# Tiles of 32 rows by 128 columns in place of 32 by 32 for two thin products of an RWKV block

## The chip, the cores and the metric

The kernel runs on one core of a Trainium2 chip. The metric is the device time of one execution, in microseconds (us); the number given for a kernel is the median of its runs. The engines of the core are called by the profile's names: PE (TensorE, matrix products; PEld are its weight loads), DVE (VectorE), ACT (ScalarE), POOL (GpSimd) and SP (SyncE, which issues DMA transfers).

## The reference

The reference is one block of an RWKV-6 layer in float32, for 8 sequences of 256 tokens with 512 channels. What matters here is the part ahead of the scan:

```python
xn = _ln(x, ln1_w, ln1_b)
sx = _token_shift(xn, state[:, i1])
xxx = jnp.tanh((xn + sx * maa_x) @ maa_w1).reshape(b, l, 5, 1, EXTRA_MAA)
xxx = jnp.matmul(xxx, maa_w2).reshape(b, l, 5, E)
x5 = xn[:, :, None] + sx[:, :, None] * (maa_stack + xxx)
w = jnp.exp(-jnp.exp(time_decay + jnp.tanh(x5[:, :, 1] @ decay_w1) @ decay_w2))
r = (x5[:, :, 3] @ Wr.T).reshape(b, l, H, S)
k = (x5[:, :, 0] @ Wk.T).reshape(b, l, H, S)
v = (x5[:, :, 2] @ Wv.T).reshape(b, l, H, S)
g = jax.nn.silu(x5[:, :, 4] @ Wg.T)
```

There are five mixes, the "mix groups". Each has its own 32 hidden channels (EXTRA_MAA = 32) and its own matrix `maa_w2[g]` of 32 x 512. So the product behind the tanh is thin: it sums over 32 channels and yields 512. After this part come a scan over the tokens with a 16 x 16 state in each of 32 heads, a group norm, the gate, the product with Wo, and a feed-forward block.

## The kernel before, in words

Channels lie on the 128 partitions and tokens along the free axis, so a sequence is four blocks of 128 channels by 256 tokens, held as two tiles (q = 0, 1) of two blocks (m = 0, 1). For every sequence b there are three stages: `inputs_of_scan` (normalising, mixing, projections), `scan`, and `rest`. Stages of neighbouring sequences overlap.

The code doesn't issue instructions directly. It adds pieces of work to a plan (`Plan.add`), each with an engine, an assumed time, the buffers that it writes and reads, and a function that issues it. `Plan.order` sorts the pieces by a list of ranks written out by hand (`TURNS`), assumed times and free buffers, and fixes for each engine the order of its pieces and for each piece its buffers. After that the order on every engine is static. On PE a piece also has a mode: "rows32", "rows64", "columns", "turn" (transposes) or "any". The mode of the neighbours decides for an "any" piece whether it is issued as four matmuls of 128 rows by 32 columns (`narrow`) or as one of 128 by 128. There are six general PSUM tiles (`ps`) of 128 partitions by 512 float32.

The helper `mul` (line 395; its matmul is line 398, which is the line that the profile shows for nearly all products) splits a product of 128 output channels into pieces of n columns of weights:

```python
def mul(out, w, x, first=True, final=True, tiles=None):
    n = 32 if (narrow if tiles is None else tiles) else P
    for i in range(0, P, n):
        nc.tensor.matmul(out[i : i + n], lhsT=w[:, i : i + n], rhs=x, start=first, stop=final)
```

Three callers set `tiles`, so that they always use 32 columns, whatever the mode:

- `mixed` (line 653, the product at line 667) makes four of the five mixes. The weights `mw2a` hold group g on the partitions 32g to 32g + 31; the tanh output `ta` has the same layout. For each q there is one piece ("rows32", assumed 0.875 us): for both m and the four groups 1, 0, 2, 3, one product with 32 rows, four matmuls each, 32 matmuls of 32 rows by 32 columns by 256 tokens. Each group writes a PSUM tile of its own, so a piece needs four of them. After it, for b > 0, ACT adds the group's bias in PSUM (line 674), DVE multiplies by the token shift `sx` (line 676) and POOL adds `xn` (line 686). For b = 0, where nothing else is running yet, DVE does bias and product in one instruction (line 680), and two of the PSUM places come from the wide buffer `wrep`.
- `mixed_last` (line 692, the product at line 700) makes the fifth mix. Its weights `mw2b` are four copies of the group's matrix, one in each quarter of the partitions, so that the four blocks k can use four quarters: one piece of 16 matmuls of 32 by 32 by 256 (assumed 0.45 us), into four PSUM tiles.
- The decay product (line 743, "rows64") has 64 rows: 16 matmuls of 64 by 32 by 256.

Two other pieces appear in the prediction. Line 862 gathers the scan's output (matmuls of 128 by 32), after which DVE adds it (line 868). Line 903 occurs only in the last sequence: for both m and both q one matmul of 64 rows by 128 columns by 256 tokens, issued directly and not through `mul`.

Of the kernel before, what the change touches and what calls it, by code (L numbers as in the profile page):

```python
# [12 lines left out]
P = 128  # L13
# [324 lines left out]
def tile_rwkv_block(  # L338
# [33 lines left out]
    def const(name, shape):  # L372
        return plan.fixed(sb.tile(shape, F32, tag=name, name=name), name)
# [8 lines left out]
    def new(pool, name):  # L382
        return Buf(pool, name, VIEWS.get(pool, lambda t: t))
# [6 lines left out]
    def pe(us, outs, ins, emit, mode="any", into=()):  # L390
        plan.add("PE", us, outs, ins, emit, mode, into)

    narrow = False

    def mul(out, w, x, first=True, final=True, tiles=None):
        n = 32 if (narrow if tiles is None else tiles) else P
        for i in range(0, P, n):
            nc.tensor.matmul(out[i : i + n], lhsT=w[:, i : i + n], rhs=x, start=first, stop=final)  # L398

    def act(n, out, ins, emit, table=None, pointers=0):  # L400
        plan.add("ACT", 0.1 + n * 0.00084 + 0.09 * pointers, [out], ins, emit, table)

    def dve(n, outs, ins, emit, each=1.05):
        plan.add("DVE", 0.065 + n * each / 1e3, outs, ins, emit)

    def gp(n, out, ins, emit, each=1.86):
        plan.add("POOL", 0.1 + n * each / 1e3, [out], ins, emit)
# [3 lines left out]
    w1, w2a, w2b = const("mw1", [P, NK, 6 * MAA]), const("mw2a", [P, E]), const("mw2b", [P, E])  # L411
    dw1, dw2 = const("dw1", [P, NK, DEC]), const("dw2", [2 * DEC, E])
# [37 lines left out]
    def col(name, k):  # L450
        i = VECS.index(name)
        return vec()[:, k, i : i + 1]
# [17 lines left out]
    def pieces(tiles):  # L470
        return [Part(t, lambda t, i=i: t[:, i, :]) for t in tiles for i in range(2)]
# [140 lines left out]
    def project(w, src, q, name, into):  # L612

        ps = new("ps", name)
        for m in range(2):
            o = (2 * q + m) * P

            def mm(m=m, o=o):
                for k in range(NK):
                    mul(ps()[:, m, :], w[k]()[:, o : o + P], src[k // 2]()[:, k % 2, :], k == 0, k == NK - 1)  # L620

            pe(1.728, [ps], [*w, *src], mm, into=[into])
        return ps

    def project_tokens(w, src, n, name, into):

        ps = new("ps", name)
        for h in range(2):

            def mm(h=h):  # L630
                for k in (2 * h, 2 * h + 1):
                    mul(ps().rearrange("p m t -> p (m t)"), src[h]()[:, k % 2, n * P : (n + 1) * P], w[k](), k == 0, k == NK - 1)

            pe(1.72, [ps], [*src, *w], mm, into=[into])
        return ps

    def inputs_of_scan(b, got):
        xn, sx = normed(load_x(b, "xt"), 1, 1, b, b == 0)
        xin = shifted(xn, sx, "maa_x", f"xin{b}", b == 0)
        px, ta, tb = new("ps", f"psx{b}"), new("ta", f"ta{b}"), new("tb", f"tb{b}")  # L640
# [3 lines left out]
        for ks in turns:  # L644

            def mm(ks=ks):
                for k in ks:
                    mul(px()[:, 0, :], w1()[:, k, 0:P], xin[k // 2]()[:, k % 2, :], k == begin, k == end)

            pe(0.432 * len(ks), [px], [w1, *dict.fromkeys(xin[k // 2] for k in ks)], mm, into=[ta])  # L650
        act(256, ta, [px], lambda: nc.scalar.activation(ta(), px()[:, 0, :], AF.Tanh), "exp")

        def mixed():

            groups = (1, 0, 2, 3)
            x5 = {g: [new("mix", f"x5_{b}_{g}_{q}") for q in range(NQ)] for g in groups}
            ps = {(g, q): new("ps", f"psm{b}_{g}_{q}") for g in groups for q in range(NQ)}
            if b == 0:
                wide = new("wrep", f"psm{b}")
                ps.update({(g, 0): Part(wide, lambda t, i=i: t[:, 2 * i : 2 * i + 2, :]) for i, g in enumerate(groups[:2])})  # L660
            for q in range(NQ):

                def mm(q=q):
                    for m in range(2):
                        for g in groups:
                            rows, k = slice(g * MAA, (g + 1) * MAA), 2 * q + m
                            mul(ps[g, q]()[:, m, :], w2a()[rows, k * P : (k + 1) * P], ta()[rows, :], tiles=True)

                pe(0.875, [ps[g, q] for g in groups], [ta, w2a], mm, "rows32", [x5[g][q] for g in groups])
                for g in groups:  # L670
                    t, p_ = x5[g][q], ps[g, q]
                    if b:
                        for m in range(2):
                            act(256, p_, [p_, vec], lambda g=g, q=q, m=m, p_=p_: nc.scalar.activation(  # L674
                                p_()[:, m, :], p_()[:, m, :], AF.Identity, bias=col(f"maa_{g}", 2 * q + m)), pointers=1)
                        dve(512, [t], [p_, sx[q]], lambda q=q, t=t, p_=p_: nc.vector.tensor_tensor(
                            t(), p_(), sx[q](), ALU.mult))
                    else:
                        for m in range(2):
                            dve(256, [t], [p_, vec, sx[q]], lambda g=g, q=q, m=m, t=t, p_=p_: nc.vector.scalar_tensor_tensor(  # L680
                                t()[:, m, :], p_()[:, m, :], col(f"maa_{g}", 2 * q + m), sx[q]()[:, m, :], ALU.add, ALU.mult), 1.28)
                    if b == 0 and g == 2:
                        dve(512, [t], [t, xn[q]], lambda q=q, t=t: nc.vector.tensor_tensor(
                            t(), t(), xn[q]()[:, :, 1 : T + 1], ALU.add))
                    else:
                        gp(512, t, [t, xn[q]], lambda q=q, t=t: nc.gpsimd.tensor_tensor(  # L686
                            t(), t(), xn[q]()[:, :, 1 : T + 1], ALU.add))
            if b == 0:
                dve(4, [wide], [], lambda: nc.vector.memset(wide()[:, :, 0:1], 0.0))
            return x5  # L690

        def mixed_last():

            ts = [new("mix", f"x5_{b}_4_{q}") for q in range(NQ)]
            ps = [new("ps", f"psm{b}_4_{k}") for k in range(NK)]

            def mm():
                for k in range(NK):
                    rows = slice(k * MAA, (k + 1) * MAA)
                    mul(ps[k]()[:, 0, :], w2b()[rows, k * P : (k + 1) * P], tb()[rows, :], tiles=True)  # L700

            pe(0.45, ps, [tb, w2b], mm, "rows32", ts)
            for q, t in enumerate(ts):
                for m in range(2):
                    k, p_ = 2 * q + m, ps[2 * q + m]
                    if b:
                        act(256, p_, [p_, vec], lambda k=k, p_=p_: nc.scalar.activation(
                            p_()[:, 0, :], p_()[:, 0, :], AF.Identity, bias=col("maa_4", k)), pointers=1)
                        dve(256, [t], [p_, sx[q]], lambda q=q, m=m, t=t, p_=p_: nc.vector.tensor_tensor(
                            t()[:, m, :], p_()[:, 0, :], sx[q]()[:, m, :], ALU.mult))  # L710
                    else:
                        dve(256, [t], [p_, vec, sx[q]], lambda q=q, m=m, k=k, t=t, p_=p_: nc.vector.scalar_tensor_tensor(
                            t()[:, m, :], p_()[:, 0, :], col("maa_4", k), sx[q]()[:, m, :], ALU.add, ALU.mult), 1.28)
                gp(512, t, [t, xn[q]], lambda q=q, t=t: nc.gpsimd.tensor_tensor(t(), t(), xn[q]()[:, :, 1 : T + 1], ALU.add))
            return {4: ts}

        x5 = mixed()
        pd, hd = new("ps", f"psd{b}"), new("w", f"w{b}_0")
# [18 lines left out]
        pw = [new("ps", f"psw{b}_{q}") for q in range(NQ)]  # L737

        def mm():
            for m in range(2):  # L740
                for q in range(NQ):
                    rows, k = slice(DEC * q, DEC * q + DEC), 2 * q + m
                    mul(pw[q]()[:, m, :], dw2()[rows, k * P : (k + 1) * P], hd()[rows, 1, :], tiles=True)

        pe(0.875, pw, [dw2, hd], mm, "rows64", ws)
        for q in range(NQ):
# [14 lines left out]
        if b == 0:  # L761
# [3 lines left out]
            for m in range(2):  # L765
                ps, vo = new("ps", f"psv{b}_0_{m}"), new("vo", f"vo{b}_0_{m}")
# [17 lines left out]
        for q in range(NQ):  # L784
            t = got["g", q] = new("g", f"g{b}_{q}")
            ps = project(pieces(W["g"]), x5[4], q, f"psg{b}_{q}", t)
# [215 lines left out]
    with tc.manual_schedule():  # L1002
        for op in plan.order(phases):
            narrow = op.narrow
# [75 lines left out]
```

## Time and profile before

| | |
|---|---|
| median of 3 runs | 622.74 us (622.51 to 624.09) |
| profiled execution, span from first to last instruction | 620.2 us |
| PE / PEld busy in that span | 599.9 / 344.8 us |
| DVE / ACT / POOL busy | 543.5 / 513.0 / 518.7 us |
| granted TensorE clock, mean | 0.999 |
| matmul records on PE | 8496 |

The profile shows one execution; its time is given as the span, and what lies around the span (launch and end) is the difference to the measured time. "128*32 128x256" behind a matmul reads: 128 rows and 32 columns of weights, and a moving operand of 128 partitions by 256 elements. Every float32 matmul of the code leaves two MATMUL and two LDWEIGHTS records. A row of the timeline has the start, the length and what ran; consecutive records of one kind are merged, with their count behind an x, and in brackets stands how long the engine was idle before them and what ended that. Because matmuls are pipelined, the length of a merged row runs past the start of the next; the distance between starts is the better measure. A row of the windows has the stretch, its length, then for each engine its busy time and the number of its instructions in that stretch, the granted clock, the DMA engines' busy share and GB/s.

### The profile page before, as it was taken

To read this page: it belongs to the slowest core of one execution; us is meant where nothing else is said; L and a number is where in the kernel's file an instruction comes from. 1 tells how busy PE (TensorE), PEld (TensorE's weight loads), DVE (VectorE), ACT (ScalarE), POOL (GpSimd) and SP (SyncE) were. 2 spreads that over 40 slices of the span, in tenths; PEclk is the share of its full clock that TensorE was granted. 3 is DMA by queue.
4 is the path that set the end of the run, shared out by engine and by line. 5 is a ranking of instruction groups with operands and counts; after the bars stand their busy time and mean duration, and the time that the engine had idled before them with its cause. 6 is when DMAs were issued, how large, how long until landed. Compare 5 with 4: busy or idle time off the path is not lost.

```text
span 620.2 us, 20062 instructions
## 1 busy us (share of the span) xinstructions
PE 599.9 (97%) x8496; PEld 344.8 (56%) x8496; DVE 543.5 (88%) x490; ACT 513.0 (83%) x1164; POOL 518.7 (84%) x414
## 2 busy tenths in 40 slices
PE   5999999899999999999999999999999999999997
PEld 5675656456534664357543665475754464547464
DVE  5689999899999999799889999999998999895441
ACT  3888679989999999989999888899889789965441
POOL 1799999899989998899889999989889998887030
PEclk9999999999999999999999999999999999999999
DMA  8896769596768678758687797687866698961542
GB/s 294 261 247 165 216 178 230 145 246 171 208 190 237 199 194 227 197 154 226 193 248 195 220 227 201 167 240 216 223 182 193 185 248 218 262 195 65 168 141 85
DMA packets 52504, 124.91 MB, mean 201 GB/s; under 512 B 5824, under 2 KB 11200, under 8 KB 52416
## 3 DMA queue, kind: packets, MB, share of 16 engines
q1 hardware_dynamic: 48048, 119.46, 70.0%
q10 hardware_dynamic: 4368, 4.20, 2.1%
q8 instruction: 66, 1.08, 0.8%
q14 instruction: 22, 0.18, 0.1%
HBM read 115.25 MB, written 8.39 MB: 199 GB/s over the span
## 4 chain that ended last, share of the span: by engine, by line
PE 72%; ACT 13%; DVE 6%; issue 3%; DMA 2%; POOL 2%; SPq 0%; ACTq 0%; DVEq 0%; POOLq 0%
PE ps L398 60%; PE ps L862 7%; DVE st L851 3%; PE ps L574 2%; ACT sq L917 2%; DMA Ws<-in_wo 2%; PE ps L726 2%; ACT rk L917 1%; DVE vs L849 1%; ACT L787 1%; ACT mix L605 1%; DMA Ws<-in_wv 1%; POOL st L854 1%; ACT att L812 1%; ACT vs L842 1%
## 5 line engine op out<-in xcount | busy, mean ns | idle before, releaser
L851 DVE TENSOR_TENSOR_SCAN st<-wrep,vs 128x1024 f32<-128x1024 f32 x128 | 289.6, 2281 | 4.4 <-ACT wrep L832 1.2
L854 POOL TENSOR_TENSOR st<-st,r 128x1024 f32<-128x1024 f32 x128 | 254.4, 2003 | 12.1 <-DVE st L851 11.8
L849 DVE TENSOR_TENSOR vs<-vs,ps 128x1024 f32<-128x1024 f32 x122 | 144.0, 1210 | 10.5 <-ACT vs L842 9.2
L398 PE MATMUL ps<-Ws,mix 128*32 128x512 f32 (+2 forms) x864 | 114.9, 589 | 1.0 <-ACT o L952 0.7
L398 PEld LDWEIGHTS ps<-Ws,mix 128*32 128x32 f32 (+1 forms) x864 | 37.9, 116 | 64.6 <-issue 58.9
L686 POOL TENSOR_TENSOR mix<-mix,xn 128x512 f32<-128x512 f32 x62 | 66.5, 1092 | 4.1 <-DVE mix L680 2.2
L588 POOL TENSOR_TENSOR sx<-xn 128x512 f32<-128x512 f32 x30 | 31.7, 1068 | 37.7 <-ACT xn L584 37.6
L862 PE MATMUL ps<-st,con 128*32 128x256 f32 x1024 | 61.7, 380 | 0.1
L398 PE MATMUL ps<-mix,Wr 128*32 128x256 f32 (+1 forms) x760 | 59.7, 380 | 0.9 <-issue 0.9
L398 PE MATMUL ps<-mix,Wv 128*32 128x256 f32 (+1 forms) x688 | 59.7, 380 | 0.0
L398 PE MATMUL ps<-mix,Wk 128*32 128x256 f32 (+1 forms) x952 | 58.6, 379 | 0.2 <-ACT tb L734 0.2
L398 PE MATMUL ps<-Ws,g 128*32 128x512 f32 (+1 forms) x464 | 56.7, 593 | 2.0 <-POOL g L928 1.6
L398 PE MATMUL ps<-mix,Wg 128*32 128x256 f32 (+1 forms) x712 | 58.5, 379 | 0.0
L398 PE MATMUL ps<-mix,Ws 128*32 128x256 f32 (+1 forms) x736 | 57.7, 380 | 0.7 <-issue 0.4
L674 ACT ACTIVATE ps<-ps,vec 128x256 f32<-128x256 f32 x112 | 46.8, 447 | 6.7 <-PE ps L398 5.3
L607 POOL TENSOR_TENSOR mix<-mix,xn 128x512 f32<-128x512 f32 x44 | 47.5, 1092 | 5.4 <-ACT mix L605 5.3
L398 PEld LDWEIGHTS ps<-mix,Wr 128*32 128x32 f32 (+1 forms) x760 | 39.0, 119 | 18.8 <-issue 3.1
L398 PEld LDWEIGHTS ps<-mix,Ws 128*32 128x32 f32 (+1 forms) x736 | 39.3, 120 | 17.7 <-ACT o L952 1.6
L398 PEld LDWEIGHTS ps<-mix,Wv 128*32 128x32 f32 (+1 forms) x688 | 40.8, 123 | 14.9 <-issue 1.0
L812 ACT COPY att<-ps 32x256 f32<-32x256 f32 x128 | 46.6, 364 | 2.9 <-POOL g L928 0.8
L398 PEld LDWEIGHTS ps<-mix,Wg 128*32 128x32 f32 (+1 forms) x712 | 39.4, 122 | 16.3 <-issue 0.8
L862 PEld LDWEIGHTS ps<-st,con 128*32 128x32 f32 x1024 | 33.0, 110 | 27.3 <-issue 5.9
(123 smaller groups left out, 965.4 us busy)
## 6 DMA issues: line engine op xcount, KB each, us to landing
vs<-vo SPq DMA_DIRECT2D x128, 512.0 KB, 5.5
Ws<-in_fr SPq DMA_DIRECT2D x16, 512.0 KB, 5.9
Ws<-in_wo SPq DMA_DIRECT2D x16, 512.0 KB, 5.6
Ws<-in_fk SPq DMA_DIRECT2D x16, 512.0 KB, 5.5
Ws<-in_fv SPq DMA_DIRECT2D x16, 512.0 KB, 5.3
x<-in_x SPq DMA_DIRECT2D x9, 512.0 KB, 6.2
vo<-v ACTq DMA_DIRECT2D x15, 256.0 KB, 4.4
out<-o SPq DMA_DIRECT2D x15, 256.0 KB, 4.9
```

The source lines that it names most:

```text
L398: nc.tensor.matmul(out[i : i + n], lhsT=w[:, i : i + n], rhs=x, start=first, stop=final)
L574: nc.tensor.transpose(ps()[:, m, n * P : (n + 1) * P], xh[n]()[:, k * P : (k + 1) * P], idt())
L588: take(512, [sx], [xn], lambda xn=xn, sx=sx, e=nc.vector if alone and q else nc.gpsimd: e.tensor_tensor(sx(), xn()[:, :, 0:T], xn()[:, :, ...
L607: gp(512, t, [t, xn[q]], lambda q=q, t=t: nc.gpsimd.tensor_tensor(t(), t(), xn[q]()[:, :, 1 : T + 1], ALU.add))
L674: act(256, p_, [p_, vec], lambda g=g, q=q, m=m, p_=p_: nc.scalar.activation(p_()[:, m, :], p_()[:, m, :], AF.Identity, bias=col(f"maa_{g}" ...
L686: gp(512, t, [t, xn[q]], lambda q=q, t=t: nc.gpsimd.tensor_tensor(t(), t(), xn[q]()[:, :, 1 : T + 1], ALU.add))
L812: act(350, atts[q], [pc], lambda i=32 * (2 * q + m), m=m, q=q, h=32 * h: nc.scalar.copy(atts[q]()[h : h + 32, m, :], pc()[i : i + 32, 0, :]))
L849: dve(4 * T, [vs], [vs, kp], lambda m=m, vs=vs, kp=kp: nc.vector.tensor_tensor(vs(), vs(), kp()[:, m : m + 1, :].to_broadcast([P, 4, T]), ...
L851: dve(4 * T, [st], [w, vs], lambda w=w, vs=vs, st=st: nc.vector.tensor_tensor_scan(st().rearrange("p n t -> p (n t)"), w().rearrange("p n ...
L854: gp(4 * T, st, [st, r], lambda m=m, st=st, r=r: nc.gpsimd.tensor_tensor(st(), st(), r()[:, m : m + 1, :].to_broadcast([P, 4, T]), ALU.mul ...
L862: nc.tensor.matmul(pat()[32 * i : 32 * i + 32, 0, :], lhsT=con()[:, s : s + 32], rhs=done[i]()[:, j, :], start=(j == 0), stop=(j == 3),)
L917: act(256, rsb, [rs], lambda blk=2 * q + n, n=n, rows=rows, rsb=rsb: nc.scalar.copy(by_block(rsb)[rows, n, :], rs()[32 * blk : 32 * blk + ...
```

## The change

The argument `tiles` of `mul` becomes a number of columns in place of a yes or no. The two products of the mix groups pass 128, so that each product with 32 rows is one matmul of 32 rows by 128 columns and not four of 32 by 32. The decay product passes 32, which is what it had. The pieces, their assumed times, modes, buffers and order are untouched.

```diff
     def mul(out, w, x, first=True, final=True, tiles=None):
-        n = 32 if (narrow if tiles is None else tiles) else P
+        n = tiles or (32 if narrow else P)
         for i in range(0, P, n):
             nc.tensor.matmul(out[i : i + n], lhsT=w[:, i : i + n], rhs=x, start=first, stop=final)
...
-                            mul(ps[g, q]()[:, m, :], w2a()[rows, k * P : (k + 1) * P], ta()[rows, :], tiles=True)
+                            mul(ps[g, q]()[:, m, :], w2a()[rows, k * P : (k + 1) * P], ta()[rows, :], tiles=128)
...
-                    mul(ps[k]()[:, 0, :], w2b()[rows, k * P : (k + 1) * P], tb()[rows, :], tiles=True)
+                    mul(ps[k]()[:, 0, :], w2b()[rows, k * P : (k + 1) * P], tb()[rows, :], tiles=128)
...
-                    mul(pw[q]()[:, m, :], dw2()[rows, k * P : (k + 1) * P], hd()[rows, 1, :], tiles=True)
+                    mul(pw[q]()[:, m, :], dw2()[rows, k * P : (k + 1) * P], hd()[rows, 1, :], tiles=32)
```

## Prediction

> **What bounds the kernel now.** I read the page's busy table first, then the chain that ended last.
>
> ```profile
> PE 599.9 (97%) x8496; PEld 344.8 (56%) x8496; DVE 543.5 (88%) x490; ACT 513.0 (83%) x1164; POOL 518.7 (84%) x414
> ...
> PE 72%; ACT 13%; DVE 6%; issue 3%; DMA 2%; POOL 2%; SPq 0%; ACTq 0%; DVEq 0%; POOLq 0%
> ```
>
> TensorE is busy nearly all the time and carries 72% of the chain. But three other engines stand above 80%, and the second half of the argument is about them. How tight the balance is shows in the windows by stage; of each row, the first number after the length is PE's busy time, the third DVE's, the fifth POOL's.
>
> ```profile
> 40.00:100.00 60.00, 58.93 (x1237) 34.93 (x1239) 58.09 (x49) 46.38 (x104) 60.00 (x41) 1.00 0.78 198
> ...
> 160.00:220.00 60.00, 60.00 (x938) 30.24 (x931) 58.55 (x51) 57.25 (x137) 56.43 (x47) 1.00 0.77 218
> 220.00:280.00 60.00, 58.79 (x860) 30.35 (x859) 52.91 (x43) 55.61 (x127) 54.17 (x44) 1.00 0.69 185
> 280.00:340.00 60.00, 59.80 (x845) 31.89 (x848) 55.08 (x46) 56.52 (x129) 53.33 (x42) 1.00 0.78 217
> 340.00:400.00 60.00, 60.00 (x944) 34.20 (x940) 58.48 (x49) 52.94 (x130) 56.76 (x49) 1.00 0.76 205
> 400.00:525.00 125.00, 123.63 (x1732) 70.98 (x1728) 120.64 (x97) 111.10 (x245) 112.98 (x85) 1.00 0.79 213
> ```
>
> PE comes first in each stage but the first, where POOL is full, yet in three stages of 60 us (from 40, 160 and 340) DVE has under 2 us free: 1.91, 1.45 and 1.52. From 220 to 340 it has 7.09 and 4.92. So a microsecond taken from PE is worth a microsecond in the loose stages and less in the tight ones. The granted clock is 1.00 everywhere and plays no part.
>
> **What the touched products cost now.** The groups by line and form give the two products that change; for b = 0 another 32 records write into the wide buffer, so the first product has 1024 records.
>
> ```profile
> L398 PE MATMUL ps<-ta,mw2a 32*32 32x256 f32 x992 | 24.0, 385 | 0.3
> ...
> L398 PE MATMUL ps<-tb,mw2b 32*32 32x256 f32 x256 | 5.8, 386 | 1.9 <-ACT r L757 1.9
> ```
>
> The code issues 8 batches x 2 pieces x 32 = 512 matmuls of the first kind, so each leaves two records, and one piece is 64 records. Busy time is no price for a pipelined engine; start to start is. The timeline of TensorE around two such pieces (start, length, what):
>
> ```profile
> 38.77 2.11 PE L398 MATMUL ps<-mix,Wv 128*128 128x256 f32 x9
> 40.80 1.50 PE L398 MATMUL ps<-ta,mw2a 32*32 32x256 f32 x64
> 42.23 3.66 PE L398 MATMUL ps<-mix,Wr 128*32 128x256 f32 x64
> 45.70 3.64 PE L398 MATMUL ps<-mix,Wk 128*32 128x256 f32 x64
> 49.27 1.80 PE L398 MATMUL ps<-ta,mw2a 32*32 32x256 f32 x64
> 51.00 1.29 PE L398 MATMUL ps<-mix,Wg 128*32 128x256 f32 x20
> ```
>
> Between 42.23 and 45.70 the 64 records of 128*32 run four column groups side by side: 16 steps in 3.47 us, 0.217 us a step. A piece of 64 records in 16 places of the array should take four such steps, 0.87. It takes 42.23 - 40.80 = 1.43, and the second 1.73. About 0.09 of this is the change of tile shape (nine 128*128 records, 9 x 0.217 = 1.95, occupy 2.03 before 40.80). For the rest, look at this piece's weight loads in three windows; the second number is how many were running in each:
>
> ```profile
> 40.80:41.23 0.43, 0.34 (x33) 1.00 0.91 186
> 41.23:41.44 0.21, 0.10 (x1) 1.00 0.94 224
> 41.44:41.87 0.43, 0.37 (x30) 1.00 1.12 291
> ```
>
> The first half's 32 loads go in at once; then for 0.21 us one load runs, and the second half's come in a trickle of 30 over 0.43. The piece is held by the rate at which 64 loads and 64 matmuls are brought up, not by the array.
>
> **The change, part by part.** A piece of the first product becomes 8 matmuls, 16 records; the second product's 16 matmuls become 4, 8 records. So 1024 + 256 records become 256 + 64, and PE's count falls from 8496 to 7536. The arithmetic, the PSUM buffers, the order of the four groups and the planner's costs stay, so every engine's order stays and nothing moves past a queue. The third edit keeps the decay product at 32 columns, because the argument now holds a number of columns: cost nothing, no instruction changes.
>
> The trace has no matmul of 32 rows by 128 columns. The nearest row is the last batch's 64 rows by 128 columns (line 903), which has eight records in two row groups, so each row group runs four in a row, exactly as many as each of the four row groups will after the change. Its instructions (minimum, median and longest in ns), with the present loads, and its place in the timeline:
>
> ```profile
> L903 PEld LDWEIGHTS ps<-sq,con x8: 183/186/187, 575.4 to 576.0; 64*128 64x128 f32 x8
> L903 PE MATMUL ps<-sq,con x8: 376/376/480, 575.4 to 576.2; 64*128 64x256 f32 x8
> ```
> ```profile
> L398 PEld LDWEIGHTS ps<-ta,mw2a x992: 101/104/106, 15.6 to 464.4; 32*32 32x32 f32 x199
> ```
> ```profile
> 575.44 1.14 PE L903 MATMUL ps<-sq,con 64*128 64x256 f32 x8 [0.38 <-DVE sq L895]
> 576.51 0.70 PE L398 MATMUL ps<-Ws,mix 128*128 128x512 f32 x1
> ```
>
> It takes 576.51 - 575.44 = 1.07 us from its first matmul to the next piece's. Four steps are 0.87, the exposed first load is about 480 - 376 = 0.10, the change of shape 0.09: 1.06. Loads of 128 columns take 186 ns against 104, and still only the first shows. I take 1.07 for the new piece. Below, it can't go under 0.87 + 0.09 = 0.96; above, the rivals price it. The Trainium skill ("TensorE: Matmul & The Clock Gate", section "LDWEIGHTS (loading the stationary operand)") counts a load by its columns, an estimate of 107 ns for 128 against 27 for 32; that speaks against this change, and by the rows here the difference is 82 ns, paid once a piece. The same page ("Measured speedup vs the span model") has 3.07 times for four row tiles and 10.6 for sixteen small ones; by these, four row tiles take (4/3.07)/(16/10.6) = 0.86 of the sixteen, so that the piece would be an estimated 1.23 instead of 1.07 and PE's sum below an estimated 3 us.
>
> Now the saving, 1.43 - 1.07 = 0.36 a piece. Where the pieces lie, by the windows of that weight tile (64 records a piece; of the rows left out, the four stages from 160 to 400 hold 128 each like the last row, the one from 100 none):
>
> ```profile
> 0.00:40.00 40.00, 2.81 (x128) 1.00 0.91 270
> 40.00:100.00 60.00, 6.28 (x256) 1.00 0.78 198
> ...
> 400.00:525.00 125.00, 2.99 (x128) 1.00 0.79 213
> ```
>
> From 40: four pieces, 4 x 0.36, and 0.30 more for the piece of 1.73, 1.74 in all. From 160, 280, 340 and 400: two pieces each, 0.72. From 220: two, but one of them buys nothing, because PE then waits for ScalarE:
>
> ```profile
> 246.62 1.49 PE L398 MATMUL ps<-ta,mw2a 32*32 32x256 f32 x64
> 248.80 1.06 PE L398 MATMUL ps<-Ws,mix 128*32 128x512 f32 x8 [0.69 <-ACT o L952]
> ```
>
> so 0.36 there. At the start the two pieces run back to back and DVE waits for the first:
>
> ```profile
> 16.96 1.27 DVE L680 SCALAR_TENSOR_TENSOR mix<-ps,vec,sx 128x256 f32<-128x256 f32 x3 [2.17 <-PE ps L398]
> ```
>
> It gets its tile about 0.3 sooner, and the chain runs through it, so 0.3. The second product:
>
> ```profile
> 27.55 0.73 PE L398 MATMUL ps<-tb,mw2b 32*32 32x256 f32 x32
> 28.21 1.93 PE L398 MATMUL ps<-mix,Wk 128*32 128x256 f32 x32
> ```
>
> It takes 0.66 now, and with two records less in each row group than line 903 it would take 1.07 - 2 x 0.217 = 0.64. Its bounds are 0.53 (two steps and a change of shape) and 0.74 (the longer load shown in full); eight pieces save 0.16, between +1.0 and -0.6.
>
> PE's sum: 0.3 + 1.74 + 4 x 0.72 + 0.36 + 0.16 = 5.4 us.
>
> What is late next? DVE waits for the chain that these pieces feed (matmul, bias on ScalarE, product on DVE), and for the gathering matmuls behind them:
>
> ```profile
> DVE mix L676 <- ACT ps L674: 7.1, 11, 1.9
> ...
> DVE att L868 <- PE ps L862: 6.8, 6, 3.5
> ```
>
> These 13.9 us are what a faster PE can turn into time; the rest of DVE's work doesn't shrink. In the tight stages (1.74 + 0.72 + 0.72 = 3.18) and from 400 (0.72, DVE free 4.36 in 125) I let half pass: 1.95. This half is a choice; PE and DVE are both nearly full there, and neither row decides between nothing and all. From 220 to 340 (0.36 + 0.72) and at the start (0.3) all passes: 1.38. Of the second product's 0.16, half. Together 3.4 us.
>
> **Rivals.** (1) The other engines swallow it. The piece shrinks to 1.07, but DVE and POOL set the tight stages and the stretch from 400, and only 1.38 passes: 621.4. For it: POOL 60.00 of 60 from 40 to 100. Against it: DVE's 13.9 us of waits behind PE.
>
> (2) Each record waits for its own weights, so the 0.10 of the first load is paid four times: 1.07 + 3 x 0.10 = 1.37 a piece, a saving of 0.06, 0.8 in all, of which half passes: 622.3. Against it: the eight records of line 903 fit in 1.07, and the nine 128*128 records above keep 0.217 each with 128-column loads. The Trainium skill has such a rule on the page named above ("The mechanism"): a load runs beside matmuls in flight only if its row group differs. In a row group of its own every load here would be exposed; these two rows disagree with it.
>
> (3) The slower side: the four row groups share one path for weights, so that loads follow one another. From the two load rows, 82 ns for 96 more columns is 0.85 ns a column, 109 ns for 128. Sixteen loads in turn are 1.74 us and set the piece once they need over 1.43 - 0.30 = 1.13 (0.30 for the last record and the change of shape), 71 ns each: the piece would take 2.05, 0.62 more, and the second product 0.87 + 0.30 = 1.17, 0.51 more. 14 x 0.62 + 8 x 0.51 = 12.8 on PE, nearly all passed on since PE leads: about 634. Against it: line 903's two row groups started eight such loads within 0.6 us (575.4 to 576.0), where eight in turn need seven gaps of 0.11, 0.76. But two groups are not four.
>
> **How the numbers follow.** The profiled execution has a span of 620.2 us; the median of the runs is 622.74, so 2.5 lie outside the span and stay. I predict 622.74 - 3.4 = 619.3, a span of 616.8. Chances: the forecast 0.70, its own range from all of 5.4 passing (617.3) to 620.8; rival 1 0.18; rivals 2 and 3 0.06 each. A measurement here can tell 0.3%, 1.9 us. The forecast is all faster, of rival 1 a ninth: 0.72. The rest of rival 1 with rival 2 is no change, 0.22. Rival 3 is slower, 0.06. The range goes from 617.2 to 622.2: it leaves out rivals 2 and 3 and a little at the low end.
>
> **What would show it.** Right: PE x7536; groups of 32*128 with 256 and 64 records, mean about 0.40 us, loads of about 186 ns; start to start about 1.07 in the piece after 40 us and 0.64 for the second product; DVE's wait at L676 below 7.1. Rival 1: the same pieces, but PE's own waits grow by what the pieces saved. Rival 2: records of one row group 0.32 apart. Rival 3: loads that start 0.1 apart across row groups and pieces of about 2 us. The prediction is wrong if the piece stays above 1.3, or if a stage that lost PE work keeps its length with DVE idle as before.

## The result and the profile after

| | before | after |
|---|---|---|
| median of the runs compared | 624.09 us (622.51 to 624.91, 5 runs) | 617.55 us (617.27 to 618.20, 5 runs) |
| profiled execution, span | 620.2 us | 615.5 us |

The ratio is 0.9905 with a 95% interval of 0.9887 to 0.9923: 5.9 us faster (4.8 to 7.1). The prediction was 619.3, 3.4 us faster than the 622.74 then on record, with 617.2 to 622.2 as its range. The direction was right and the result lies at the fast end.

The page of the changed kernel, its busy times and its chain:

```profile
PE 593.4 (96%) x7536; PEld 343.3 (56%) x7536; DVE 542.3 (88%) x490; ACT 511.7 (83%) x1164; POOL 517.9 (84%) x414
...
PE 60%; ACT 15%; DVE 8%; POOL 8%; issue 4%; DMA 4%; SPq 0%; ACTq 0%; DVEq 0%; POOLq 0%
```

The record count is the expected 7536. PE's share of the chain fell from 72% to 60%: other engines now carry part of what PE carried. The groups of the two products by line and form, then the durations of the first one (minimum, median, longest, in ns):

```profile
L398 PE MATMUL ps<-ta,mw2a 32*128 32x256 f32 x248 | 18.2, 400 | 0.2
...
L398 PE MATMUL ps<-tb,mw2b 32*128 32x256 f32 x64 | 5.7, 426 | 1.9 <-ACT r L757 1.9
```
```profile
L398 PEld LDWEIGHTS ps<-ta,mw2a x248: 181/185/185, 15.0 to 459.2; 32*128 32x128 f32 x124
L398 PE MATMUL ps<-ta,mw2a x248: 374/374/479, 15.1 to 459.4; 32*128 32x256 f32 x124
```

The median matmul is as long as before (374), and the longest stands 105 ns above it: only the first load of a piece shows, as in line 903. The timeline of PE at the two pieces of b = 1, and at the first piece of the second product:

```profile
37.83 2.10 PE L398 MATMUL ps<-mix,Wv 128*128 128x256 f32 x9
39.86 1.15 PE L398 MATMUL ps<-ta,mw2a 32*128 32x256 f32 x16
40.94 3.66 PE L398 MATMUL ps<-mix,Wr 128*32 128x256 f32 x64
44.42 3.64 PE L398 MATMUL ps<-mix,Wk 128*32 128x256 f32 x64
48.03 1.15 PE L398 MATMUL ps<-ta,mw2a 32*128 32x256 f32 x16
49.11 3.23 PE L398 MATMUL ps<-mix,Wg 128*32 128x256 f32 x56
```
```profile
26.62 0.71 PE L398 MATMUL ps<-tb,mw2b 32*128 32x256 f32 x8
27.27 1.50 PE L398 MATMUL ps<-mix,Wk 128*32 128x256 f32 x24
```

From start to start a piece of the first product takes 1.08 us in both places (1.43 and 1.73 before), one of the second 0.65.

Where did the time come from? The table sets the start of the same pieces in the two traces side by side; the last column is how far the changed kernel is ahead.

| piece | before, us | after, us | ahead, us |
|---|---|---|---|
| first product, b = 0 (the first changed work) | 15.56 | 15.05 | 0.51 |
| first product, b = 1, first piece | 40.80 | 39.86 | 0.94 |
| b = 2, first piece | 76.75 | 74.92 | 1.83 |
| b = 2, second piece | 92.86 | 89.38 | 3.48 |
| second product, b = 2 | 117.24 | 114.35 | 2.89 |
| second product, b = 3 | 203.05 | 199.55 | 3.50 |
| first product, b = 4, second piece | 257.72 | 254.47 | 3.25 |
| b = 5, first piece | 318.06 | 314.40 | 3.66 |
| b = 5, second piece | 328.33 | 324.65 | 3.68 |
| b = 6, second piece | 391.04 | 386.64 | 4.40 |
| b = 7, second piece | 463.45 | 458.65 | 4.80 |
| second product, b = 7 | 550.18 | 545.46 | 4.72 |

The first 0.51 lies ahead of any changed instruction, so it is the difference of two executions. Between the two pieces of b = 2 the lead grows by 1.65, far more than a piece's 0.35. The timeline of the kernel before shows why:

```profile
78.17 1.50 PE L398 MATMUL ps<-mix,Wr 128*32 128x256 f32 x23
80.60 2.54 PE L398 MATMUL ps<-mix,Wr 128*32 128x256 f32 x41 [0.94 <-issue]
82.79 3.80 PE L398 MATMUL ps<-mix,Wg 128*32 128x256 f32 x64
```

and after the change, the same work:

```profile
76.00 3.66 PE L398 MATMUL ps<-mix,Wr 128*32 128x256 f32 x64
79.47 3.64 PE L398 MATMUL ps<-mix,Wg 128*32 128x256 f32 x64
```

The 64 records of the r projection took 4.62 us before and 3.47 after. PE stood in the middle of an accumulation and waited for nothing that the profile shows. 3.47 is the pace of the array, so 1.15 us of the lead at this place comes from a wait that has nothing to do with the array time of a piece; the experiments look into it. It isn't all kept. At line 862, which gathers the scan's output, the kernel before goes on without a wait, and the changed kernel stands for GpSimd (before, then after):

```profile
94.29 3.66 PE L398 MATMUL ps<-mix,Wg 128*32 128x256 f32 x64
97.76 2.04 PE L862 MATMUL ps<-st,con 128*32 128x256 f32 x32
```
```profile
93.94 0.59 PE L862 MATMUL ps<-st,con 128*32 128x256 f32 x2
95.69 1.71 PE L862 MATMUL ps<-st,con 128*32 128x256 f32 x27 [1.16 <-POOL st L854]
```

The lead is 3.82 us where PE comes to line 862, and 2.83 where it comes to the k projection soon after (106.47 before, 103.64 after the change).

### The profile page after: what moved, and what is told of

It is laid out like the page before. It is cut to its first block, busy times and chain, and to the rows that moved or that the text cites. A ratio compares the mean times of both kernels' runs of the same rounds, so it can differ in the third digit from the quotient of the medians.

```text
span 615.5 us, 18121 instructions
## 1 busy us (share of the span) xinstructions
PE 593.4 (96%) x7536; PEld 343.3 (56%) x7536; DVE 542.3 (88%) x490; ACT 511.7 (83%) x1164; POOL 517.9 (84%) x414
## 4 chain that ended last, share of the span: by engine, by line
PE 60%; ACT 15%; DVE 8%; POOL 8%; issue 4%; DMA 4%; SPq 0%; ACTq 0%; DVEq 0%; POOLq 0%
PE ps L398 50%; PE ps L862 6%; POOL st L854 4%; DVE st L851 4%; PE ps L574 2%; ACT rk L917 2%; ACT sq L917 2%; DMA Ws<-in_wo 2%; PE ps L726 2%; DVE vs L849 2%; POOL mix L686 2%; ACT att L812 1%; DMA vs<-vo 1%; ACT wrep L832 1%; DVE sq L895 1%
## 5 line engine op out<-in xcount | busy, mean ns | idle before, releaser
L849 DVE TENSOR_TENSOR vs<-vs,ps 128x1024 f32<-128x1024 f32 x122 | 143.7, 1205 | 9.7 <-ACT vs L842 8.4
L398 PEld LDWEIGHTS ps<-mix,Ws 128*32 128x32 f32 (+1 forms) x736 | 40.7, 120 | 16.8 <-ACT o L952 1.5
```

The lines of the kernel that those rows point to most:

```text
L849: dve(4 * T, [vs], [vs, kp], lambda m=m, vs=vs, kp=kp: nc.vector.tensor_tensor(vs(), vs(), kp()[:, m : m + 1, :].to_broadcast([P, 4, T]), ...
```

## The experiments

The theory was that PE time counts: a piece of the first product is 0.35 us shorter, and most of that reaches the end. Its rivals were that the shorter stream of instructions makes the difference, that the earlier arrival of the products at ScalarE and VectorE does, and that other engines swallow the rest. Each kernel was timed against the kernel before on the same chip; a difference in us is worked out from the ratio.

**The change again.** The changed kernel as it is, beside the next three.

> The changed kernel as it is, for a direct comparison with its variants on one chip. Every theory: 5.9 us below the kernel before (ratio 0.9905), pieces of the first product 1.08 us from start to start and of the second 0.64.

617.15 us against 623.99, ratio 0.9896 (0.9880 to 0.9913): 6.5 us below before (5.4 to 7.5).

**The first product alone.**

```diff
-                    mul(ps[k]()[:, 0, :], w2b()[rows, k * P : (k + 1) * P], tb()[rows, :], tiles=128)
+                    mul(ps[k]()[:, 0, :], w2b()[rows, k * P : (k + 1) * P], tb()[rows, :], tiles=32)
```

> Only the first product (four mixes) has 128 columns; the second (fifth mix) has 32 as before. Theory, that what counts is the PE time of a piece: 16 pieces keep 1.08, the eight of the second product go back from 0.64 to 0.66, so within 0.2 us of the full change, 5.7 below before. Rival, that the gain comes from the shorter instruction stream (960 matmul records fewer gave 5.9 us, 6.1 ns each): 768 fewer, 4.7 below before.

Ratio 0.9912 (0.9896 to 0.9928), 5.5 us below before. Its pieces are 1.08 and 0.66. This is 1.0 us above the full change on the same chip, within the intervals of both, and so the run doesn't tell the theory (0.2) from the shorter stream (1.2).

**The second product alone.**

```diff
-                            mul(ps[g, q]()[:, m, :], w2a()[rows, k * P : (k + 1) * P], ta()[rows, :], tiles=128)
+                            mul(ps[g, q]()[:, m, :], w2a()[rows, k * P : (k + 1) * P], ta()[rows, :], tiles=32)
```

> Only the second product has 128 columns. Theory: its piece has 32 records before, which all go in at once, so there is no stall to take away: 0.66 becomes 0.64, in all 0.1 us, not to be told from the kernel before. Rival, the shorter stream: 192 records fewer, 1.2 us below before.

Ratio 0.9981 (0.9969 to 0.9993), 1.2 us below before (0.4 to 1.9). That is the rival's number and not the theory's, although the pieces went from 0.66 to 0.64 as expected. But its own trace doesn't show a stream that flows better. The timeline of PE has two waits without a releaser, one within a piece of the first product:

```profile
49.06 0.69 PE L398 MATMUL ps<-ta,mw2a 32*32 32x256 f32 x26
50.24 1.28 PE L398 MATMUL ps<-ta,mw2a 32*32 32x256 f32 x38 [0.48 <-issue]
...
55.35 1.24 PE L398 MATMUL ps<-mix,mw 128*32 128x256 f32 x17
57.74 0.85 PE L398 MATMUL ps<-mix,mw 128*32 128x256 f32 x12 [1.14 <-issue]
```

Counting loads and matmuls from the start of the trace, these two fall at instructions 1205 and 1459, and the one of the kernel before at 2479: 254 and 4 x 255 apart. The page's instruction queue says what such a step is; of the kernel before, then of the changed one:

```profile
q8 instruction: 66, 1.08, 0.8%
```
```profile
q8 instruction: 59, 0.97, 0.7%
```

2 x 8496 loads and matmuls in 66 packets are 257 a packet, 2 x 7536 in 59 are 255. The waits stand where one packet of instructions ends and the next must be there. The traces also hold each packet of that queue with its time. Between 35 and 96 us six of the traces have nine waits of over 0.2 us without a releaser, and each of the nine ends 1.39 to 1.54 us after a packet of 16 KB has landed. Other waits without a releaser, near 455 and 540 us, end 2.3 us or more behind the last packet; they are something else.

**64 columns.** Both products on tiles of 32 by 64.

```diff
-                            mul(ps[g, q]()[:, m, :], w2a()[rows, k * P : (k + 1) * P], ta()[rows, :], tiles=128)
+                            mul(ps[g, q]()[:, m, :], w2a()[rows, k * P : (k + 1) * P], ta()[rows, :], tiles=64)
...
-                    mul(ps[k]()[:, 0, :], w2b()[rows, k * P : (k + 1) * P], tb()[rows, :], tiles=128)
+                    mul(ps[k]()[:, 0, :], w2b()[rows, k * P : (k + 1) * P], tb()[rows, :], tiles=64)
```

> Both products with 64 columns, 32 rows: a piece of the first has 32 records in eight places, of the second 16. Theory, that a piece stalls only where its records outnumber what goes in at once (32): no stall, and the first load that shows is shorter (64 columns), so 1.02 and 0.59 a piece, 16 x 0.06 + 8 x 0.05 = 1.4 us of PE time less than with 128, about 7 us below before. Rival, that the stall belongs to tiles narrower than the array: half of the gain, 3 us below before. Rival, the shorter stream: 640 records fewer, 3.9 below before.

Ratio 0.9906 (0.9889 to 0.9924), 5.9 us below before and not to be told from the full change. Both rivals are out at 3 and 3.9; the further 1 us isn't seen. A piece:

```profile
40.01 1.12 PE L398 MATMUL ps<-ta,mw2a 32*64 32x256 f32 x32
41.06 1.29 PE L398 MATMUL ps<-mix,Wr 128*32 128x256 f32 x20
```

It takes 1.05, 0.03 less than with 128 columns, where 0.06 was expected. So 32 records in eight places run at the array's pace: the stall needs no 128 columns to go away.

**The decay product too.**

```diff
-                    mul(pw[q]()[:, m, :], dw2()[rows, k * P : (k + 1) * P], hd()[rows, 1, :], tiles=32)
+                    mul(pw[q]()[:, m, :], dw2()[rows, k * P : (k + 1) * P], hd()[rows, 1, :], tiles=128)
```

> The full change, and the decay product too on tiles of 64 rows by 128 columns: its pieces have 32 records now and 8 then. Theory, PE time of a piece: 32 records don't stall (1.02 from start to start), and the longer first load shows, 1.07, so eight pieces cost 0.4 us more: not to be told from the full change, about 6 below before. Rival, the shorter stream of instructions at 6 ns a matmul record (the run with the second product alone took out 192 records and came out 1.2 below before): another 192 fewer, about 7.2 below before.

Ratio 0.9909 (0.9891 to 0.9927), 5.7 us below before: the theory's number. Its pieces take 1.06 to 1.07 and not 1.02, as expected. Another 192 records fewer bought nothing, and the rival's 7.2 lies outside the interval (4.6 to 6.8), so the 1.2 us of the run with the second product alone can't be a price per record.

**64 records again, in eight places.**

```diff
-                    for m in range(2):
+                    for m, c in ((m, slice(h * P, h * P + P)) for m in range(2) for h in range(2)):
                         for g in groups:
                             rows, k = slice(g * MAA, (g + 1) * MAA), 2 * q + m
-                            mul(ps[g, q]()[:, m, :], w2a()[rows, k * P : (k + 1) * P], ta()[rows, :], tiles=128)
+                            mul(ps[g, q]()[:, m, c], w2a()[rows, k * P : (k + 1) * P], ta()[rows, c], tiles=64)
```

> The full change, but the first product on tiles of 32 rows by 64 columns with each matmul cut into two halves of the tokens: 64 records in a piece again as before the change, in eight places of the array, the same array time (a step is half as long, there are twice as many). Theory, that a piece stalls where its records outnumber the 32 that go in at once: about 1.4 a piece again, the time of before (less than 1 us below). Rival, that the stall belongs to tiles of 32 columns or to sixteen places: no stall, 1.05 a piece, 6 us below before.

Ratio 0.9916 (0.9896 to 0.9936), 5.2 us below before. The theory of the stall falls. A piece and its loads:

```profile
40.23 1.21 PE L398 MATMUL ps<-ta,mw2a 32*64 32x128 f32 x64
41.37 0.85 PE L398 MATMUL ps<-mix,Wr 128*32 128x256 f32 x12
```
```profile
40.23:40.45 0.22, 0.22 (x24) 1.00 0.84 168
40.45:40.66 0.21, 0.21 (x19) 1.00 1.19 263
40.66:41.18 0.52, 0.52 (x36) 1.00 0.97 260
```

64 records take 1.14 here and not 1.43. The second half does come in the same trickle, some 30 loads in 0.5 us, but there is no stretch of 0.2 us with almost no loads ahead of it, as the kernel before has one from 41.23 to 41.44. So more than 32 records cost about 0.09 by the trickle (against 1.05), and the rest of the 0.35 comes with what this run lacks: sixteen places of 32 columns, or 256 tokens a matmul (here 128). No run separates these two, and why loads pause there stays open.

**PE time put back into the piece.**

```diff
-                    for m in range(2):
+                    for m in (0, 0, 1):
```

> The full change, and in each piece of the first product the four matmuls of m = 0 run twice (the second run overwrites the first with the same values): two steps more, 1.08 + 0.43 = 1.51 a piece, with only 128 records more than in the full change. Theory, PE time: 14 pieces are 0.08 longer than before the change, so the time of before or 1 us above it. Rival, the shorter stream: 832 of the 960 records stay away, 5 us below before.

Ratio 0.9987 (0.9973 to 1.0000), 0.8 us below before (0.0 to 1.7). A piece, as expected, takes 1.51:

```profile
41.60 1.58 PE L398 MATMUL ps<-ta,mw2a 32*128 32x256 f32 x24
43.11 1.27 PE L398 MATMUL ps<-mix,Wr 128*32 128x256 f32 x17
```

With 832 of the 960 records still gone, putting the time back takes nearly all of the gain away: the shorter stream is not the cause of 5 us. It comes out about 2 us better than PE time says, though (14 x 0.08 = 1.1 above before), and its trace has no wait between instruction packets above 0.2 us.

**More instructions, same array time.**

```diff
-            op.narrow = mode == "columns"
+            op.narrow = True
```

> The full change, and every piece that may have either shape is issued as four matmuls of 32 columns (the records of 128 by 128, some 500 without the transposes, become four times as many, about 1500 more), the array time the same. Theory, PE time: nothing but some more changes of shape around transposes, 0.2 us each, 0 to 2 us above the full change, 4 to 6 below before. Rival, the stream at 6 ns a record: 9 us above the full change, 3 above before.

Ratio 0.9942 (0.9923 to 0.9962), 3.6 us below before, 2 to 3 above the full change. The theory's end, a little beyond it; 1656 records more did not cost 9 us.

**PE time elsewhere.** In `project`:

```diff
+                if name.startswith("psr"):
+                    mul(ps()[:, m, :], w[0]()[:, o : o + P], src[0]()[:, 0, :])
                 for k in range(NK):
```

> The full change, and each of the four accumulations of the r projection runs its first matmul twice (the second overwrites the first): 4 x 0.217 = 0.87 us more PE time a batch, 6.9 in all, far from the products of the mix groups. Theory, PE time is what counts: nearly all of it passes, 6 us above the full change, the time of before within 1 us. Rival, that the gain came from the earlier arrival of the mix products at ScalarE and VectorE: those stay early, at most 2 us above the full change, 4 below before.

Ratio 1.0079 (1.0065 to 1.0093), 4.9 us above before, 11 above the full change. The expectation had the padding too small: a matmul leaves two records and takes two steps, so each repeat costs 2 x 0.217, and 32 of them 13.9 us. PE's busy time has gone from 593.4 to 607.7:

```profile
PE 607.7 (97%) x7726; PEld 354.9 (57%) x7726; DVE 543.7 (87%) x490; ACT 512.3 (82%) x1164; POOL 518.2 (83%) x414
```

11 of 13.9 us pass, four fifths. The rival of the earlier arrival allowed 2 us, so as it was put it is out. The run doesn't separate the two cleanly, since all that PE does behind the padding comes later too, mix products included: the second piece of b = 1 starts at 50.60, and at 48.03 in the full change.

**Less PE time than the change leaves.** In `project`, without the first block of the r projection:

```diff
-                for k in range(NK):
-                    mul(ps()[:, m, :], w[k]()[:, o : o + P], src[k // 2]()[:, k % 2, :], k == 0, k == NK - 1)
+                for k in range(int(name.startswith("psr")), NK):
+                    mul(ps()[:, m, :], w[k]()[:, o : o + P], src[k // 2]()[:, k % 2, :], k == int(name.startswith("psr")), k == NK - 1)
```

> The full change, and the r projection leaves out its first of four blocks of channels (r is wrong by that part): 0.87 us less PE time a batch, 6.9 in all. Theory, PE still bounds most stages: 4 to 6 us below the full change, 10 to 12 below before. Rival, that VectorE and GpSimd are now the bound: 0 to 2 us below the full change.

Ratio 0.9920 (0.9908 to 0.9933), 5.0 us below before, no better than the full change. By the same correction the cut is 13.9 us, and none of it shows. The chain that ended last, and PE's longest wait behind the start:

```profile
PE 38%; ACT 30%; DVE 15%; issue 7%; POOL 6%; DMA 4%; ACTq 0%; SPq 0%; DVEq 0%; POOLq 0%
```
```profile
PE ps L398 <- ACT r L757: 2.8, 1, 2.8
```

PE carries 38% of the chain and now waits for ScalarE, VectorE and GpSimd. Here the rival "other engines swallow it" is right in the main. A part can be the clock: it stood at half for two stretches of 3.4 us in the profiled run (last section), by which PE loses up to an estimated 3.4 us.

**The first three batches, and the last five.** Both products, by batch:

```diff
-                            mul(ps[g, q]()[:, m, :], w2a()[rows, k * P : (k + 1) * P], ta()[rows, :], tiles=128)
+                            mul(ps[g, q]()[:, m, :], w2a()[rows, k * P : (k + 1) * P], ta()[rows, :], tiles=128 if b < 3 else 32)
...
-                    mul(ps[k]()[:, 0, :], w2b()[rows, k * P : (k + 1) * P], tb()[rows, :], tiles=128)
+                    mul(ps[k]()[:, 0, :], w2b()[rows, k * P : (k + 1) * P], tb()[rows, :], tiles=128 if b < 3 else 32)
```

The other kernel has 32 and 128 exchanged.

> The change in the first three batches only. PE time alone: 0.3 at the start, four pieces of 0.36 behind it, 1.7 us below before. Theory, that the early stretch (35 to 95 us) also loses waits of PE for its instructions, gaps at every 256th record or a multiple of it, which three traces with the longer stream show there (0.9 to 1.9 us) and the full change doesn't: 2.5 to 3.5 below before.

Ratio 0.9940 (0.9928 to 0.9953), 3.7 us below before (2.9 to 4.5), where PE time alone gives 1.7.

> The change in the last five batches only. PE time alone: nine pieces of 0.36 and little else, 3.2 us below before. Theory, that waits for instructions stay in the early stretch as before: 2.5 to 3.2 below before, a trace with gaps between 35 and 95 us, and runs that spread as widely as those of before (3 us; the full change 1.3). With the run of the first three batches it adds up to the full change's 5.9 to 6.5, against 4.9 by PE time alone.

Ratio 0.9946 (0.9932 to 0.9960), 3.4 us below before (2.5 to 4.2), PE time alone 3.2. The two add up to 7.1, against 5.9 and 6.5 for the whole. The spread of its runs was 1.2 us and not 3, a miss. But its trace has the wait in the r projection of b = 2, at the same count of instructions (2479) as the kernel before:

```profile
78.78 1.50 PE L398 MATMUL ps<-mix,Wr 128*32 128x256 f32 x23
80.89 2.53 PE L398 MATMUL ps<-mix,Wr 128*32 128x256 f32 x41 [0.61 <-issue]
83.07 1.26 PE L398 MATMUL ps<-mix,Wg 128*32 128x256 f32 x19
```

and the trace with the first three batches changed has none. So by the medians about 2 us of the gain belong to the early stretch beyond the shorter pieces (1.7 when the 0.30 within the long piece is counted with them). The traces don't show these 2 us. In the one with the first three batches the first changed work starts at 15.15 and the second product of b = 2 at 114.42, 0.41 and 2.82 ahead of the kernel before: 2.4 gained, where the shorter pieces and the 0.30 make 2.0. PE waits for GpSimd at line 862 there too (1.14). With the last five batches changed, that product starts at 117.45, 0.21 behind, and the end comes 2.4 ahead (617.8 against 620.2): 2.6 gained. The two make 5.0, near the 4.9 of PE time alone. That the waits between instruction packets go away in the early stretch is seen in the traces; that they make up the 2 us of the medians isn't shown.

## Why the prediction was right, and where it was off

- **The new piece, 1.07 and 0.64.** Measured 1.08 and 0.64 to 0.65. Line 903 was the right row: four records in a row for each row group, one load exposed, one change of shape. Four row groups load side by side as two do. The reason given for the old 1.43 was right only in part: 64 records in eight places take 1.14, so bringing up 64 loads and matmuls costs 0.09 of the 0.35.
- **Two rules of the Trainium skill.** Rival 2 came from the rule that a load runs beside matmuls in flight only if its row group differs ("TensorE: Matmul & The Clock Gate", section "The mechanism"). The changed kernel doesn't follow it: loads of 185 ns within one row group, and still 16 records in 1.08. The same section of the Trainium skill also lets a load into the background weight buffer be pulled ahead, and that the prediction left out; the trace fits it, but doesn't show which buffer a load goes to. The same page's speedups for four row tiles and sixteen small ones made an estimated 1.23; the trace has 1.08.
- **PE's sum, 5.4 us.** It holds for the pieces but leaves out a term on each side. The wait in the r projection stood in the profile of before (0.94 with no releaser, 1.15 with what goes with it), and I counted only its smaller sister, the 0.30 within the piece of 1.73, which stands at a border of packets too (instruction 1205). The traces of the changed kernel have neither. On the other side stands the new wait for GpSimd at line 862, 1.16, in the stage where GpSimd had 60.00 of 60. In the profiled execution the two nearly cancel: at 117 us 2.4 is gained since the first changed work (2.89 - 0.51), and the sum for these batches is 2.0.
- **The half that passes in the tight stages.** This is the term that was mis-sized. Between 117 and 203 us the lead grows by 0.6 of the 0.7 offered, between 328 and 391 by all 0.7. The 13.9 us of VectorE's waits, which were to show what can pass, are no measure of it: 12.7 are still there. Line 868 waits 6.9 in place of 6.8, and line 676 in all 5.8 in place of 7.1, only under other names:

```profile
DVE mix L676 <- ACT ps L674: 2.7, 6, 1.0
...
DVE mix L676 <- issue: 1.9, 1, 1.9
...
DVE mix L676 <- POOL att L919: 1.2, 1, 1.2
```

  The last two are the waits near 250 us that the trace of before puts down to ScalarE (1.92 and 1.18). What was lost was lost elsewhere: 0.6 between 93 and 117 us beside the gain of a piece, with the wait for GpSimd and, in both kernels, one of 1.9 for ScalarE; a whole piece at three places (b = 4 first, which was forecast, b = 5 first, b = 7 first) where PE runs into its next wait; and what the last piece gained at 531 us, where PE waits 1.40 us for the weights of Wo and waited 0.43 before. The clearest of these places is in a stage that I had called loose; after the change

```profile
314.40 1.15 PE L398 MATMUL ps<-ta,mw2a 32*128 32x256 f32 x16
315.84 2.37 PE L398 MATMUL ps<-mix,Ws 128*32 128x256 f32 x40 [0.29 <-ACT mix L943]
```

  and before

```profile
318.06 1.49 PE L398 MATMUL ps<-ta,mw2a 32*32 32x256 f32 x64
319.50 2.80 PE L398 MATMUL ps<-mix,Ws 128*32 128x256 f32 x48
```

  where the next work starts 1.44 after the piece in both, because it needs ScalarE's squared tile. An engine's free time over a stage said little; whose output the next piece on PE needs, and how long it has been there, would have said it.
- **The sum against one profiled execution.** 4.7 us lie between the two spans, of which 0.5 ahead of any changed instruction; 5.9 lie between the runs. The timed runs of the kernel before had spans from 619.8 to 623.5, 621.6 in the median of 43; the profiled 620.2 is from their low end. Those of the changed kernel were 615.0 to 616.4 (11 runs). So 1 to 2 us of the gain can't be found in these two traces. Of those 43 runs, 14 had a mean granted clock of 0.996 or 0.997, and their median time is 624.0 us against 623.3 of the others; none of the 11 runs of the changed kernel had it. That can make a few tenths, and no trace shows such a run. The forecast of 3.4 lies outside the measured 4.8 to 7.1, and it is in part luck that the range, whose fast end is all of PE's sum, still takes in a gain that has another 1 to 2 us of unknown source.
- **Rival 1** was wrong for the whole of this change, though its sign, a new wait of PE, shows at line 862; it was right in the main for the next: a cut of 13.9 us more on PE gains nothing. **Rival 3** was refuted by the pieces of 1.08.
- **A misreading of the stages.** PE does not come first from 100 to 160 us: VectorE had 57.90 and GpSimd 56.87 there against 56.69. No piece of the first product lies in that stage, so the sum doesn't change.

What stays open: the 1.2 us of the second product alone, the pause of 0.2 us before the second half of a 16-place piece, and the 1 to 2 us by which the timed runs gain more than the traces, most of it, by the medians, with the first three batches.

## What to carry to other kernels

Price a tile shape from start to start, not from busy time, and compare with records divided by the places that run side by side; where a piece of many small tiles falls short of the array's pace, fewer and wider tiles give it back at the cost of one longer first load. Look for the nearest instruction in the trace with the same number of records in a row on each row group: it priced the new piece to 0.01 us. And before letting a fixed share of a gain pass, ask piece by piece what the next work on the engine waits for.

## What the runs showed of the hardware

- PE waits at borders of instruction packets, some 255 loads and matmuls apart, for up to 1.1 us, in the stretch from 35 to 96 us. Waits of over 0.2 us there appear in the traces with the longer stream (before, the second product alone, eight places with 64 records, the last five batches) and in those of 64 columns and of all narrow; the full change, its repeat and the others have none. Each of these waits ends 1.39 to 1.54 us after a packet of 16 KB has landed.
- Loads take 101, 127 and 181 ns at least for 32, 64 and 128 columns of 32 rows, 0.83 ns a column.
- Taking work from PE can slow its clock: where the r projection was cut, the mean granted clock was 0.994 in all five runs. The windows of the profiled one, with the granted clock behind the five engines:

```profile
90.00:100.00 10.00, 7.80 (x114) 3.87 (x110) 7.93 (x7) 6.92 (x15) 10.00 (x7) 0.87 0.86 224
100.00:110.00 10.00, 10.00 (x183) 6.29 (x179) 10.00 (x9) 8.53 (x17) 9.63 (x8) 0.96 0.72 206
110.00:116.00 6.00, 4.12 (x79) 2.51 (x67) 4.03 (x4) 5.82 (x14) 5.30 (x4) 1.00 0.54 130
116.00:125.00 9.00, 8.07 (x96) 3.89 (x100) 8.27 (x8) 8.76 (x23) 7.73 (x7) 0.81 0.62 147
```

  After its 2.8 us of waiting the clock was 0.81 over 9 us, 3.4 us at half speed (from 117.9). Another 3.4 us at half speed, from 97.4, follow two waits of 0.60 and 1.60 us with a few matmuls between them. The Trainium skill ("TensorE: Matmul & The Clock Gate", section "What's actually happening") halves the clock after an idle window of about 3.4 us and restores it after a busy one. The trace agrees with the length of the half speed; no single wait here was as long as that window.
